# Attention projections of a two-layer kernel: eight block products replaced by seven, with weight sums prepared ahead

## The chip, the cores and the metric

The kernel runs on one core of one Trainium2 chip. The metric is the device time of one execution in microseconds (us). A kernel is run several times and the median counts; one more execution is recorded by the hardware profiler, and all durations below come from that one. The engines are named as in the profile: PE multiplies matrices, PEld is its weight load, DVE does elementwise work, ACT does elementwise functions, POOL and SP issue DMAs here.

## What is computed

Two attention layers follow each other, on four images of 32 x 32 tokens with 768 channels and 12 heads of 64. Cut to what matters:

```
for layer in (0, 1):
    xn  = group_norm(x)                    # 32 groups of channels
    q, k, v = xn @ Wq + bq, xn @ Wk + bk, xn @ Wv + bv
    if layer == 1:                         # depthwise 3x3 convolution and layer norm of each
        q, k, v = [layer_norm(dwconv3x3(t)) for t in (q, k, v)]
    a   = softmax(q @ k.T / 8 + rel_h(q) + rel_w(q))     # per image and head, 1024 x 1024
    o   = a @ v        (+ q in layer 1)
    x   = x + o @ Wp + bp                  # the projection that this change touches
```

All arrays are fp32. The projection of one image and layer is a product of a 768 x 768 matrix with 768 x 1024 outputs of attention (channels by tokens).

## The kernel before

All work stands in one long function, `two_layers`. Channels lie on the 128 partitions, so 768 channels are six tiles (NC = 6) of 128, and the 1024 tokens of an image are two halves of 512. A *stage* is one image in one layer. The eight stages run in the order: images 0 and 1 in layer 0, images 0 and 1 in layer 1, then images 2 and 3 likewise. A stage has six *pairs*, each a pair of heads (128 channels); 48 pairs in all, numbered from 0.

**The order is written out by hand.** PE, DVE, ACT and POOL execute exactly what the Python program emits, in that order; only SP's DMAs are placed by the scheduler. `attend` (L663) is a generator for one pair. For each half of the queries it does two groups of four key tiles: scores (L724, L726), exponentials (L731), running sums of them on DVE (L738, L740), then the product with V (L746), called AV here. It yields twice after the four score tiles and twice after AV, so a pair has 16 *steps*: steps 0 and 1 of each four stand between scores and AV, steps 2 and 3 between AV and the next scores. The dictionary `events` says what else is emitted at which step, relative to the start of a stage: Q, K and V of the next pair, convolution taps (L506, L508), norms, loads, mixes, projections. The loop at the end of `two_layers` walks through steps and events.

**PSUM** has eight banks: scores use one fixed double bank and two places (`place_b`, `place_c`) of two banks each; between scores these places are handed out as single banks by `bank` (L119) in a rotating order, with one further small bank that also serves the sum over keys, `z` (L688).

**Seven products for Q, K and V.** In layer 0, from the third pair on, `sevens` (L355) already computes two 128-channel blocks at once by seven products of quarters (Strassen's scheme): the contraction of six tiles is cut into two times three, the tokens into two halves. It needs five sums of token quarters (`mix_tokens`, L272) and five sums of weight quarters for each of nine pairs of blocks. `mix_weights` (L256) makes the latter once, in stage 0: it loads two weight tiles, writes each of five sums (L268) into a tile `x` of which there are two, and stores it to DRAM (`mixed`, L269). Loading and summing are emitted in the same step. The steps are listed near the end of `two_layers` (steps 2, 4, 18, 34, 36, 50, 56, 60, 66).

**The projection** `project` (L758) of stage k is emitted in stage k+1, in steps 7 to 14. For each of six output tiles m it loads the weights (L764), and for each half of the tokens it loads the residual x (L776), makes one product over six tiles of attention outputs (L131, called from L779, out tile `proj`), adds bias and residual on DVE (L780) and stores (L781). A product is six calls of `halves` (L128), each of which issues two matmuls of 128 x 64 weights with 512 columns; the profile lists each of these as two instructions. In layer 1 of image 0 a bias is first computed on PE from the weights (`pbias`, L770). The last stage's projection has no stage after it and is emitted after the last pair, with a check of all softmax sums (L838 to L844) in between; this stretch is called the tail below.

Of the kernel before, what the change touches and what calls it, by code (L numbers as in the profile page):

```python
# [9 lines left out]
F32 = mybir.dt.float32  # L10
# [3 lines left out]
ALU = mybir.AluOpType  # L14
# [3 lines left out]
P = 128  # L18
B = 4
S = 32  # L20
T = S * S
C = 768
NC = C // P
D = 64
HALF = T // 2
# [6 lines left out]
BIAS = (0, 24)  # L32
TAPS = 48
LN = 75
# [11 lines left out]
def two_layers(ctx: ExitStack, tc: tile.TileContext, keep, x_in, wqkv, wproj, rels, windows, vrow, small, const, onehot, picks, out):  # L46
# [19 lines left out]
    nc = tc.nc  # L66
    pool = lambda name, bufs, **kw: ctx.enter_context(tc.tile_pool(name=name, bufs=bufs, **kw))
    fixed = pool("fixed", 1)
    dram = pool("dram", 1, space=bass.MemoryType.DRAM)
    xnp = pool("xnp", 2)  # L70
    wp = pool("wp", 2)
    work = pool("work", 2)
    one = pool("one", 1)
# [45 lines left out]
    def bank(name):  # L119

        place = turn.pop(0)
        turn.append(place)
        return place.single(name) if place else small_bank(name)

    def small_bank(name):
        return ps_small.tile([P, 512], F32, tag="small", name=name)

    def halves(ps, a, b, start=True, stop=True, **kw):  # L128

        for lo in (0, D):  # L130
            nc.tensor.matmul(ps[lo : lo + D], a[:, lo : lo + D], b, start=start, stop=stop, **kw)  # L131
# [15 lines left out]
    def col(c, lo=0, hi=P):  # L147
        return sm[lo:hi, c : c + 1]
# [15 lines left out]
    stages = [(b0 + k, layer) for b0 in range(0, B, 2) for layer in range(2) for k in range(2)]  # L164
# [8 lines left out]
    weights = {}  # L173

    N_SUMS = 5
    mixed = [dram.tile([P, N_SUMS, NC // 2, P], F32, tag=f"mixed{u}", name=f"mixed{u}") for u in range(NC + NC // 2)]
    mixed_there = set()


# [3 lines left out]
    def part(at, n):  # L183
        return shared[:, at : at + n]
# [24 lines left out]
    for i, (_, layer, hp) in enumerate(items):  # L209
        first = (i - 1) * 16 + shift(i)  # L210
# [7 lines left out]

    def load_xn(stage):
        b, layer = stage  # L220
        xn = xnp.tile([P, NC, T], F32, tag="xn", name="xn")
        src = rows(mid[b] if layer else x_in[b])
        for n in range(NC):
            nc.sync.dma_start(xn[:, n, :], src[:, n, :])
        xns[stage] = xn

    def two(i, s):

        hp = items[i][2]
        return ((hp, 0), (hp, 1)) if s == 0 else ((hp, 2), (hp + 1, 2))  # L230

    def load_weights(n):

        if n >= len(uses):
            return
        i, s, *some = uses[n]
        _, layer, hp = items[i]
        w = wp.tile([P, NC, P], F32, tag="wqkv", name="wqkv_t")
        weights[uses[n]] = w
        if not some:  # L240
            nc.sync.dma_start(w, wqkv[layer, hp, :, s])
        elif some[0] == 0:
            (pa, sa), (pb, sb) = two(i, s)
            nc.sync.dma_start(w[:, :3, :], wqkv[0, pb, :, sb, 3:])
            nc.sync.dma_start(w[:, 3:, :], wqkv[0, pa, :, sa, :3])
        else:
            u = hp if s == 0 else NC + hp // 2
            assert u in mixed_there
            sums = slice(2 * some[0] - 2, min(2 * some[0], N_SUMS))
            n_sums = sums.stop - sums.start  # L250
            nc.sync.dma_start(w[:, : 3 * n_sums, :].rearrange("p (a n) c -> p a n c", n=3), mixed[u][:, sums])

    def used(use):
        load_weights(uses.index(use) + 2)

    def mix_weights(u):  # L256

        (pa, sa), (pb, sb) = two(u, 0) if u < NC else two(2 * (u - NC), 2)
        a = wp.tile([P, NC, P], F32, tag="wproj", name="mix_a")
        nc.sync.dma_start(a, wqkv[0, pa, :, sa])  # L260
        b = wp.tile([P, NC, P], F32, tag="wproj", name="mix_b")
        nc.sync.dma_start(b, wqkv[0, pb, :, sb])
        a1, a2, b1, b2 = a[:, :3, :], a[:, 3:, :], b[:, :3, :], b[:, 3:, :]
        sums = (b1, b2, ALU.add), (a1, a2, ALU.add), (a1, b2, ALU.add), (a2, b2, ALU.subtract), (b1, a1, ALU.subtract)
        for n, (x, y, op) in enumerate(sums):
            to = wp.tile([P, HALF], F32, tag="x", name="mix")
            to = to[:, : 3 * P].rearrange("p (n c) -> p n c", c=P)
            nc.vector.tensor_tensor(to, x, y, op)  # L268
            nc.sync.dma_start(mixed[u][:, n], to)  # L269
        mixed_there.add(u)  # L270

    def mix_tokens(stage):  # L272

# [53 lines left out]
    pbias = fixed.tile([P, NC], F32, tag="pbias", name="pbias")  # L327
# [333 lines left out]
    rest, found = [], ()  # L661
# [95 lines left out]

    def project(stage, os):  # L758

        b, layer = stage  # L760
        src, dst = rows(mid[b] if layer else x_in[b]), rows(out[b] if layer else mid[b])
        for m in range(NC):
            w = wp.tile([P, NC, P], F32, tag="wproj", name="wproj_t")
            nc.sync.dma_start(w, wproj[layer, :, :, m, :].rearrange("h p q -> p h q"))  # L764
            bias = col(BIAS[layer] + 18 + m)
            if layer:
                if b == 0:
                    ps = small_bank("pbias")
                    for n in range(NC):
                        nc.tensor.matmul(ps[:, 0:1], w[:, n, :], col(LN + 5), start=(n == 0), stop=(n == NC - 1))  # L770
                    nc.vector.tensor_tensor(pbias[:, m : m + 1], ps[:, 0:1], bias, ALU.add)
                bias = pbias[:, m : m + 1]
            for h in range(2):
                cols = slice(h * HALF, (h + 1) * HALF)
                x = wp.tile([P, HALF], F32, tag="x", name="x")
                nc.sync.dma_start(x, src[:, m, cols])  # L776
                ps = bank("proj")
                for n in range(NC):
                    halves(ps, w[:, n, :], os[n][:, cols], n == 0, n == NC - 1)  # L779
                nc.vector.scalar_tensor_tensor(x, ps, bias, x, ALU.add, ALU.add)  # L780
                nc.sync.dma_start(dst[:, m, cols], x)  # L781
                yield


    events = {}

    def at(step, piece):
        events.setdefault(step, []).append(piece)

    n_steps = NKT * (T // QC)  # L790
    oss = [[] for _ in stages]
    for k in range(1, len(stages)):
        first = (k - 1) * NC * n_steps
        at(first + n_steps, lambda k=k: load_xn(stages[k]))
        norm = group_norm(stages[k])
        for r in range(12):
            at(first + 2 * n_steps + 2 + 3 * r, lambda norm=norm: next(norm, None))
        if stages[k][1] == 0:
            mix = mix_tokens(stages[k])
            for r in range(5):  # L800
                step = 5 * n_steps + r // 3 if stages[k - 1][1] else 4 * n_steps + 4 + r // 2
                at(first + step, lambda mix=mix: next(mix, None))
        elif stages[k - 1][1] == 0:
            at(first + 4 * n_steps + 6, lambda: [nc.gpsimd.memset(pad, 0.0) for pad in pads])
    mix = mix_tokens(stages[0])
    for r in range(5):
        at(12 + r // 2, lambda mix=mix: next(mix, None))

    for u, step in ((2, 2), (7, 4), (3, 18), (4, 34), (8, 36), (5, 50), (0, 56), (6, 60), (1, 66)):
        at(step, lambda u=u: mix_weights(u))  # L810
    pairs = [Pair(i) for i in range(len(items))]
    for i, pair in enumerate(pairs):
        for r, piece in pair.plan():
# [1 line left out]
    for n in range(2):  # L815
        load_weights(n)
    for k, stage in enumerate(stages):
        steps = project(stage, oss[k])
        first = (k + 1) * NC * n_steps
        for r in range(2 * NC):  # L820
            at(first + 7 + 2 * r // 3, lambda steps=steps: next(steps, None))
    for _ in group_norm(stages[0]):
        pass
    for step in sorted(e for e in events if e < 0):
# [2 lines left out]
    step = 0  # L827
    for i, pair in enumerate(pairs):
        for _ in attend(pair, oss[i // NC]):
            for piece in events.pop(step, ()):  # L830
                piece()
            step += 1
    for part in rest:
        found = part(*found)
    def check():

        total = stat.tile([P, 1], F32, tag="total", name="total")
        nc.vector.tensor_reduce(total, seen, AX.X, ALU.add)  # L838
        good = stat.tile([P, 1], F32, tag="good", name="good")
        nc.vector.tensor_scalar(good, total, LIMIT, None, ALU.is_lt)  # L840
        ps = small_bank("good")
        nc.tensor.matmul(ps[:1, :1], cst[:, ONES : ONES + 1], good, start=True, stop=True)
        bad = keep.tile([1, 1], mybir.dt.int32, tag="bad", name="bad")
        nc.vector.tensor_scalar(bad, ps[:1, :1], -1.0, 1.0 * P, ALU.mult, ALU.add)  # L844
        return bad

    last = [piece for step in sorted(events) for piece in events.pop(step)]
    for piece in last[:2]:
        piece()
    bad = check()  # L850
    for piece in last[2:]:
        piece()
    for place in (place_b, place_c):
        place.close()
    return bad
# [288 lines left out]
```

## Time and profile before

| what | value |
|---|---|
| median of three runs | 3959.64 us (3958.61 to 3959.95) |
| the profiled execution's own time | 3959.69 us |
| its span | 3957.8 us |
| granted PE clock, mean | 0.997 |
| matmuls of the projection, `proj` | 2304 instructions |
| matmuls of Q, K and V by six tiles, `qkv` | 3648 instructions, 815.6 us busy |
| DVE: running sums of exponentials (L740) | 576, 705.6 us busy |
| DVE: convolution taps (L508) | 576, 758.4 us busy |
| DVE: bias and residual (L780) | 96, 72.1 us busy |
| load of projection weights | 48 of 384 KB, 3.7 us to landing |
| load of x from `mid`, store to `out` | 48 each of 256 KB, 2.7 and 3.2 us to landing |
| store of x to `mid` | 48 of 256 KB, 3.7 us to landing |
| load of weight sums | 66 of 384 KB, 3.1 us, and 33 of 192 KB, 2.3 us |

A line of groups in the profile reads: line of the kernel, engine, operation, output tile <- input tiles, shape, count | busy us, mean ns of one | idle time of the engine just before, and what ended it. Matmuls overlap each other, so the mean of one (593 ns) is longer than the distance from one to the next. A line of windows has the length of the window, then for PE, PEld, DVE, ACT and POOL the busy us with the number of instructions, then granted clock, share of the DMA engines and GB/s. A line of the timeline has the start, the duration, the instructions, and in brackets how long the engine had been idle and who ended that.

### The profile page before, as it was taken

How to read it: one execution, taken by the hardware profiler on the slowest of the kernel's cores; microseconds unless marked ns; L12 is line 12 of the kernel's file. 1: busy time of each engine (PE TensorE's matmuls, PEld its weight loads, DVE VectorE, ACT ScalarE, POOL GpSimd, SP SyncE). 2: the span in 40 equal slices, each digit the busy share in tenths (PEclk: the TensorE clock that was granted, in tenths of full speed). 3: DMA queues.
4: the chain of work that ended last, by engine and by line, in shares of the span. 5: the costliest groups of instructions: out<-in, count | busy, mean ns of one | idle time of the engine just before them, and what ended most of it. 6: DMA issues, size and time to landing. Idle time of an engine off the chain costs nothing.

```text
span 3957.8 us, 79930 instructions
## 1 busy us (share of the span) xinstructions
PE 3884.8 (98%) x35026; PEld 1743.2 (44%) x35026; DVE 2492.4 (63%) x2794; ACT 1835.7 (46%) x2717; POOL 411.4 (10%) x776
## 2 busy tenths in 40 slices
PE   7999999999999999999899999999999999999999
PEld 3535534534344444444445355355443444434443
DVE  2456424558489984799633554245675998848883
ACT  2454424555255552455423554254542555525551
POOL 0111100110000100000011110001100011000010
PEclk9999999999999999999999999999999999999999
DMA  5333242221411312212133222423124112131122
GB/s 161 85 115 113 77 135 75 65 55 50 130 46 35 87 43 84 62 44 70 43 104 90 59 72 64 147 59 76 44 59 124 38 46 52 44 103 44 38 48 76
DMA packets 179044, 293.33 MB, mean 74 GB/s; under 512 B 22528, under 2 KB 77952, under 8 KB 178688
## 3 DMA queue, kind: packets, MB, share of 16 engines
q1 hardware_dynamic: 117248, 187.41, 15.1%
q0 software_dynamic: 61440, 100.71, 11.1%
q8 instruction: 279, 4.57, 0.5%
q14 instruction: 77, 0.63, 0.1%
HBM read 153.36 MB, written 34.01 MB: 47 GB/s over the span
## 4 chain that ended last, share of the span: by engine, by line
PE 88%; DVE 9%; DMA 1%; issue 1%; ACT 0%; POOL 0%; DVEq 0%; SPq 0%; ACTq 0%
PE qkv L131 18%; PE s L724 16%; PE av L746 15%; PE proj L131 13%; PE m3m L131 4%; PE s L726 4%; PE m1m L131 4%; PE m4m L131 4%; DVE shared L508 3%; PE rel L566 3%; PE ln_c L131 3%; PE z L688 2%; DVE acc L740 2%; PE m L131 2%; PE ln_t L544 1%
## 5 line engine op out<-in xcount | busy, mean ns | idle before, releaser
L731 ACT ACTIVATE e<-s 128x1024 f32<-128x1024 f32 x768 | 776.1, 1024 | 447.5 <-PE s L726 414.0
L131 PE MATMUL qkv<-xn,wqkv_t 128*64 128x512 f32 x3648 | 815.6, 597 | 7.2 <-DVE gmean L300 4.1
L740 DVE TENSOR_TENSOR acc<-acc,e 128x1024 f32<-128x1024 f32 x576 | 705.6, 1225 | 183.7 <-ACT e L731 132.7
L724 PE MATMUL s<-q,k 64*128 64x512 f32 x3072 | 810.8, 604 | 4.3 <-ACT e L731 3.5
L508 DVE SCALAR_TENSOR_TENSOR shared<-shared,sm 128x1056 f32<-128x1056 f32 x576 | 758.4, 1317 | 14.9
L726 PE MATMUL s<-bias,ones 64*128 64x512 f32 x1536 | 612.8, 790 | 10.0 <-DMA bias<-high 7.1
L746 PE MATMUL av<-e,vt 128*64 128x512 f32 x2624 | 594.2, 595 | 0.0
L593 POOL DMA_DIRECT2D bias<-high x384 | 204.2, 552 | 3271.6 <-ACT high L582 3023.5
L131 PE MATMUL proj<-q,wproj_t 128*64 128x512 f32 x2304 | 504.2, 593 | 0.2 <-DVE bad L844 0.2
L131 PEld LDWEIGHTS qkv<-xn,wqkv_t 128*64 128x64 f32 x3648 | 253.9, 137 | 491.8 <-issue 481.4
L491 ACT ACTIVATE shared<-qkv,sm 128x512 f32<-128x512 f32 (+1 forms) x288 | 129.1, 502 | 595.8 <-PE qkv L131 595.8
L724 PEld LDWEIGHTS s<-q,k 64*128 64x128 f32 x3072 | 281.9, 187 | 257.8 <-issue 217.0
L746 PEld LDWEIGHTS av<-e,vt 128*64 128x64 f32 x2624 | 185.0, 137 | 346.9 <-issue 320.1
L131 PEld LDWEIGHTS proj<-q,wproj_t 128*64 128x64 f32 x2304 | 163.3, 137 | 316.6 <-issue 315.8
L738 DVE TENSOR_TENSOR acc<-e 128x1024 f32<-128x1024 f32 x96 | 117.5, 1224 | 293.7 <-ACT e L731 282.4
L726 PEld LDWEIGHTS s<-bias,ones 64*128 64x128 f32 x1536 | 150.2, 188 | 195.2 <-issue 183.6
L593 POOL DMA_DIRECT2D bias<-whole x384 | 206.4, 567 | 125.4 <-DVE whole L583 115.8
L681 ACT COPY weighed<-av 128x512 f32<-128x512 f32 x96 | 56.3, 586 | 301.9 <-PE av L746 301.9
L780 DVE SCALAR_TENSOR_TENSOR x<-proj,sm,x 128x512 f32<-128x512 f32 x48 | 36.1, 751 | 217.0 <-PE proj L131 217.0
L780 DVE SCALAR_TENSOR_TENSOR x<-proj,pbias,x 128x512 f32<-128x512 f32 x48 | 36.0, 751 | 215.8 <-PE proj L131 215.8
L131 PEld LDWEIGHTS ln_c<-cst,shared 128*64 128x64 f32 x2304 | 133.3, 139 | 50.2 <-issue 42.3
L131 PE MATMUL ln_c<-cst,shared 128*64 128x128 f32 x2304 | 141.4, 277 | 8.2 <-DVE shared L508 7.5
(121 smaller groups left out, 3744.0 us busy)
## 6 DMA issues: line engine op xcount, KB each, us to landing
bias<-high POOLq DMA_DIRECT2D x384, 128.0 KB, 2.8
bias<-whole POOLq DMA_DIRECT2D x384, 128.0 KB, 3.0
wqkv_t<-in_wqkv SPq DMA_DIRECT2D x78, 384.0 KB, 3.1
wqkv_t<-mixed SPq DMA_DIRECT2D x66, 384.0 KB, 3.1
wproj_t<-in_wproj SPq DMA_DIRECT2D x48, 384.0 KB, 3.7
wqkv_t<-in_wqkv SPq DMA_DIRECT2D x66, 192.0 KB, 2.5
xn<-in_x SPq DMA_DIRECT2D x24, 512.0 KB, 7.7
x<-in_x SPq DMA_DIRECT2D x48, 256.0 KB, 2.8
```

Source lines behind the costliest of these rows:

```text
L131: nc.tensor.matmul(ps[lo : lo + D], a[:, lo : lo + D], b, start=start, stop=stop, **kw)
L491: nc.scalar.activation(self.pad[s][:, rows, there : there + src.shape[2]], src, AF.Identity, bias=col(self.column(s)))
L508: nc.vector.scalar_tensor_tensor(y, window, tap, y, ALU.mult, ALU.add)
L566: nc.tensor.matmul(ps[lo : lo + S, k * S : (k + 1) * S].rearrange("p (b c) -> p b c", b=2), rel[rows, 2 * self.layer + i, first : first + ...
L593: nc.gpsimd.dma_start(sets, some.unsqueeze(1).to_broadcast([D // 2, 2, QC]))
L688: nc.tensor.matmul(z[j * D : (j + 1) * D, :], cst[:, ONES : ONES + D], acc[:, j, :], start=True, stop=True,)
L724: nc.tensor.matmul(ps[:, j, :], k[rows, keys], q[rows, cols], start=True, stop=False)
L726: nc.tensor.matmul(ps[:, j, :], ones[rows, keys], bias[c][rows, kt // 2, :], start=False, stop=True,)
L731: nc.scalar.activation(e, ps, AF.Exp)
L738: nc.vector.tensor_tensor(acc, es[0], es[1], ALU.add)
L740: nc.vector.tensor_tensor(acc, acc, e, ALU.add)
L746: nc.tensor.matmul(av[j * D : (j + 1) * D, :], pair.vt[:, kt, j * D : (j + 1) * D], e[:, j, :], start=(kt == 0), stop=(kt == NKT - 1),)
```

## The change

The projection takes the form that `sevens` has, for two output tiles at once (`four` and `three` are its first four and last three products), and the sums of weights are made differently.

- `project` now returns three things: a call that loads the first weights, `sums`, which forms 15 sums of 128 x 512 attention outputs on DVE (nine into new space, six in place), and `products`, a generator that emits `four` and `three` for three pairs of output tiles.
- Each product is three calls of `halves`. `four` accumulates products 1 and 3 in one bank and 2 and 4 in another; ACT copies the bank after product 1, DVE adds it after product 2. `three` accumulates products 5 and 7 in one bank, DVE adding it in between, and 6 in another. A pair of output tiles has four DVE adds for the shared terms and two more in the final additions.
- The steps: in stages followed by layer 0, sums at steps 4 to 6 and products at 7, 9, 11, 13, 14, 15; in those followed by layer 1, sums at 1, 6, 8, 9, 10 and products at 9, 11, 13, 15, 17, 19. In the last stage the sums of two of three heads are put at steps 4 and 6 of the last pair, one more at step 10, and the rest after it.
- The new space is the input buffer of the same stage, which is free by then: `xnp` has two tags of one buffer in place of one tag of two. The load of the next input goes from step 16 to step 20 of a stage.
- `mix_weights` handles six more pairs of weight blocks, those of the projection (9 to 11 for layer 0, 12 to 14 for layer 1). The load is emitted some five steps ahead of the sums. Three of the five sums are written in place over their operands and stored from there. The bias `pbias` is computed there, in stage 1.

```
-    for u, step in ((2, 2), (7, 4), (3, 18), (4, 34), (8, 36), (5, 50), (0, 56), (6, 60), (1, 66)):
-        at(step, lambda u=u: mix_weights(u))
+    for u, call, step in (
+        (2, 0, 5), (7, 6, 11), (3, 13, 18), (4, 22, 29), (8, 31, 38), (5, 40, 47), (0, 49, 55), (6, 57, 63), (1, 65, 71),
+        (9, 72, 77), (10, 78, 83), (11, 84, 89), (12, 138, 143), (13, 145, 150), (14, 152, 157),
+    ):
+        mix = mix_weights(u)
+        for at_step in (call, step):
+            at(at_step, lambda mix=mix: next(mix))
...
-        sums = (b1, b2, ALU.add), (a1, a2, ALU.add), (a1, b2, ALU.add), (a2, b2, ALU.subtract), (b1, a1, ALU.subtract)
-        for n, (x, y, op) in enumerate(sums):
-            to = wp.tile([P, HALF], F32, tag="x", name="mix")
-            to = to[:, : 3 * P].rearrange("p (n c) -> p n c", c=P)
+        for n, to, x, y, op in (
+            (2, None, a1, b2, ALU.add), (4, None, b1, a1, ALU.subtract), (0, b1, b1, b2, ALU.add),
+            (1, a1, a1, a2, ALU.add), (3, a2, a2, b2, ALU.subtract),
+        ):
+            if to is None:
+                to = wp.tile([P, HALF], F32, tag="x", name="mix")
+                to = to[:, : 3 * P].rearrange("p (n c) -> p n c", c=P)
             nc.vector.tensor_tensor(to, x, y, op)
             nc.sync.dma_start(mixed[u][:, n], to)
...
-            for h in range(2):
-                cols = slice(h * HALF, (h + 1) * HALF)
-                x = wp.tile([P, HALF], F32, tag="x", name="x")
-                nc.sync.dma_start(x, src[:, m, cols])
-                ps = bank("proj")
-                for n in range(NC):
-                    halves(ps, w[:, n, :], os[n][:, cols], n == 0, n == NC - 1)
-                nc.vector.scalar_tensor_tensor(x, ps, bias, x, ALU.add, ALU.add)
-                nc.sync.dma_start(dst[:, m, cols], x)
+        def m(ps, pair, at, x, some=range(3), more=False):
+            w = weights[4 * pair + at // 2][:, 3 * (at % 2) : 3 * (at % 2) + 3, :]
+            for n in some:
+                halves(ps, w[:, n, :], x(n), start=not (n or more), stop=n == 2, skip_group_check=True)
...
+        def put(which, cols, x, ps, term=None):
+            bias = pbias[:, which : which + 1] if layer else col(BIAS[0] + 18 + which)
+            nc.vector.scalar_tensor_tensor(x, ps, bias, x, ALU.add, ALU.add)
+            if term is not None:
+                nc.vector.tensor_tensor(x, x, term, ALU.add)
+            nc.sync.dma_start(dst[:, which, cols], x)
...
+        def four(pair, n_first=3):
+
+            u, w = extra(9), extra(10)
+            b1, b2 = bank("p4p2"), bank("p3p5")
+            x21, x12 = get(2 * pair + 1, first), get(2 * pair, second)
+            m(b1, pair, 0, extra)
+            nc.scalar.copy(u, b1)
+            yield
+            m(b2, pair, 1, lambda n: extra(n + 3), range(n_first))
+            if n_first == 3:
+                add(u, u, b2)
+            m(b1, pair, 2, x11, more=True)
+            m(b2, pair, 1, lambda n: extra(n + 3), range(n_first, 3))
+            load(4 * pair + 2)
+            if n_first < 3:
+                add(u, u, b2)
+            add(w, u, b1, ALU.subtract)
+            put(2 * pair + 1, first, x21, b1)
+            m(b2, pair, 3, x22, more=True)
+            load(4 * pair + 3)
+            add(u, u, b2, ALU.subtract)
+            put(2 * pair, second, x12, b2)
+            yield
+
+        def three(pair):
+            u, w = extra(9), extra(10)
+            b3, b4 = bank("p1p6"), bank("p7")
+            x11, x22 = get(2 * pair, first), get(2 * pair + 1, second)
+            m(b3, pair, 4, lambda n: extra(n + 6))
+            add(u, u, b3)
+            m(b4, pair, 5, lambda n: os[n + 3][:, first])
+            load(4 * pair + 4)
+            put(2 * pair, first, x11, b4, u)
+            m(b3, pair, 6, lambda n: os[n][:, second], more=True)
+            load(4 * pair + 5)
+            put(2 * pair + 1, second, x22, b3, w)
...
+        if k + 1 == len(stages):
+            at(first - 12, call)
+            for r, *what in ((-12, range(5), (0,)), (-10, range(5), (1,)), (-6, (0,), (2,))):
+                at(first + r, lambda sums=sums, what=what: sums(*what))
+            continue
+        at(first + 2, call)
+        late = stages[k + 1][1]
+        for r, what in ((1, (0,)), (6, (1,)), (8, (2,)), (9, (3,)), (10, (4,))) if late else ((4, (0, 1)), (5, (2,)), (6, (3, 4))):
+            at(first + r, lambda sums=sums, what=what: sums(what))
+
+        for r, n in zip((9, 11, 13, 15, 17, 19) if late else (7, 9, 11, 13, 14, 15), (2, 1) * 3):
+            for _ in range(n):
+                at(first + r, lambda products=products: next(products))
...
+    found = rest.pop(0)(*found)
+    next(products)
     for part in rest:
         found = part(*found)
+    sums(range(1, 5), (2,))
```

`get` loads a residual tile, `load` the next weights into one of two buffers, `extra(i)` is the i-th 128 x 512 part of the new space, and `add` is a DVE addition.

## The prediction on record

> **What bounds the kernel.** I read the page's busy shares first, then the granted clock, then TensorE (PE) cut by head pair, then PE's waits. A "pair" is one of the 48 rounds of attention over two heads; its start is its first exponential, and the windows below are such rounds.
>
> ```profile
> PE 3884.8 (98%) x35026; PEld 1743.2 (44%) x35026; DVE 2492.4 (63%) x2794; ACT 1835.7 (46%) x2717; POOL 411.4 (10%) x776
> L131 PE MATMUL proj<-q,wproj_t 128*64 128x512 f32 x2304 | 504.2, 593 | 0.2 <-DVE bad L844 0.2
> ```
>
> PE is idle 73 us of 3957.8. "Busy" may hide slack, so I look at pairs with and without projection (columns: window, length, then busy of PE, weight load, DVE, ACT, POOL):
>
> ```profile
> 476.90:593.70 116.80, 116.80 (x798) 42.57 (x796) 35.40 (x39) 32.64 (x42) 8.31 (x16) 1.00 0.41 122
> 666.90:722.20 55.30, 55.30 (x513) 22.34 (x512) 33.38 (x40) 32.42 (x42) 6.41 (x13) 1.00 0.20 54
> 947.90:1085.20 137.30, 137.30 (x970) 53.83 (x968) 74.68 (x86) 44.02 (x71) 8.30 (x16) 1.00 0.34 103
> 1085.20:1160.50 75.30, 75.30 (x682) 33.21 (x680) 65.77 (x69) 42.98 (x69) 8.31 (x16) 1.00 0.22 59
> ```
>
> A layer-0 pair that carries a projection is 61.5 us longer than one that does not; in layer 1 it is 62.0. DVE has 62.6 us idle in the third window. So PE work in a projection is time, one for one. Its price is in the tail, where nothing else runs (chain of what ended last):
>
> ```profile
> 3900.56 51.74 PE proj L131 x240
> ```
>
> 51.74/240 = 0.2156 us an instruction. A stage's projection has 12 products x 6 heads x 2 halves x 2 instructions = 288, so 62.1 us, agreeing with the windows.
>
> **Part 1: seven products for eight.** Per stage: 3 pairs of output blocks x 7 products x 3 heads x 2 halves x 2 = 252 instructions, 36 fewer: 36 x 0.2156 = **7.76 us**. For the seven stages that run beside attention this is 54.3 us, if PE doesn't wait. Whether it waits is the question, since the new form lets ACT or DVE read a PSUM bank in the middle of its accumulation. The kernel already does this for Q and K (PE, a pair of stage 1; 12 instructions a product):
>
> ```profile
> 671.01 2.75 PE L131 MATMUL m4m<-xn,wqkv_t 128*64 128x512 f32 x12
> 673.58 2.75 PE L131 MATMUL m3m<-xn,wqkv_t 128*64 128x512 f32 x12
> 676.16 2.74 PE L131 MATMUL m4m<-xn,wqkv_t 128*64 128x512 f32 x12
> 678.73 2.74 PE L131 MATMUL m3m<-xn,wqkv_t 128*64 128x512 f32 x12
> ...
> 684.74 2.75 PE L131 MATMUL m1m<-shared,wqkv_t 128*64 128x512 f32 x12
> 687.32 2.75 PE L131 MATMUL m<-shared,wqkv_t 128*64 128x512 f32 x12
> 689.89 2.75 PE L131 MATMUL m1m<-shared,wqkv_t 128*64 128x512 f32 x12
> 692.57 1.13 PE L724 MATMUL s<-q,k 64*128 64x512 f32 x4
> ```
>
> Starts are 2.58 us apart: no gap at either reuse of a bank. [...]
>
> The sequence gives each reader one product's time: product 3 into bank 1 needs only ACT's copy, which has product 2 as cover; product 4 into bank 2 needs one DVE add (0.69), covered by product 3, so DVE may be 2.58 - 0.69 = 1.9 us behind; the last product likewise.
>
> *DVE's own load.* Added per stage: 15 sums of outputs and 3 x 6 adds = 33 of about 0.69 (row L707, 0.692), 22.8 us. The 12 final adds stay. In layer 0: 35 + 23 of 109 us. In layer 1: 75 + 23 of 129 us. The tightest place is the first product group of a layer-1 pair (event step 9). By my addition of rows from the pair's start, DVE ends its norm 5.8 us after PE starts the scores, then owes three acc adds (3.8), four tap steps (4.7) and six sums (4.2): it is free 18.5 us after those scores started. PE meanwhile has scores 4.4, z 1.0, centring 1.8, one padded product 5.2, transposes 2.2 and two short products 5.2, 19.8. The add is due a product later: about 3 us in hand. Later groups have more. ACT gains three copies of 0.59 a stage.
>
> *What it does cost in waits.* PE's waits at such products, from 480 to 3890 us:
>
> ```profile
> PE m4m L131 <- issue: 4.5, 3, 3.0
> PE m3m L131 <- DVE shared L376: 0.5, 1, 0.5
> ```
>
> 5.0 us over 25 groups of seven, 0.2 each, most of it in one group at the DVE-bound end of a layer-1 stage. I take 21 groups x 0.2 = **4 us** loss. Bounds: 0, and 12 layer-1 groups at that worst group's 3.6 us, 43 us.
>
> *SP's queue.* Per pair of blocks it issues five weight loads, four x loads and four stores in order, and x loads wait for a store to land (3.2 to 3.7 us), with weight loads behind them. The tightest weight load is freed after product 2 and needed after product 4: 5.2 us for a landing of 3.1. Beside attention, AV (3.4) or scores (4.4) add slack. I charge nothing; if the cover went, about 0.5 us a load.
>
> *Moves.* The next input load goes from step 16 to 20 of a stage, 14 steps (some 65 us) ahead of its first reader; its landing is 4.2 to 7.7, and on SP it stands behind the projection's last stores, which it needs in any case. POOL's queue gets nothing. One buffer for each parity now holds the sums; its last reader is step 19. The 9.0 us of bias matmuls (72 x 0.25, window 1465.8 to 1612.4 is that much longer) only move to stage 1. Nothing.
>
> **Part 2: sums of weights.** Today each of nine mixes writes five tiles through two buffers:
>
> ```profile
> DVE mix L268 <- DMA mixed<-mix: 31.6, 18, 3.9
> ```
>
> That is DVE's waits; then PE's timeline at the first long stall, and the window around it, whose last three columns are granted clock, DMA share and GB/s:
>
> ```profile
> 232.81 4.49 PE L131 MATMUL m1m<-shared,wqkv_t 128*64 128x512 f32 x12 [2.77 <-DVE shared L376]
> ```
>
> ```profile
> 231.00:239.00 8.00, 6.19 (x24) 2.08 (x24) 2.53 (x4) 2.71 (x4) 0.00 (x0) 0.79 0.72 213
> ```
>
> DVE stands for 31.6 us; where Q's adds are queued behind, PE stands too: 2.77 at 232.8, 2.98 at 321.2, 0.42 at 290.9 and 371.6, and 1.43 at 359.8, half of which I put down to it. And the two long ones are followed by a lower clock: 0.79 over 8 us is 1.7 us lost, and the 12 matmuls took 4.49, not 2.75, so 1.74 each. With three sums in place only two tiles need a buffer, both free long before. 2.77 + 2.98 + 0.84 + 0.7 + 2 x 1.74 = 10.8; I take **10.5 us**. Bounds: 5 (the new steps meet other adds) and 13 (all stalls there go). Six more mixes add 30 x 0.56 on DVE where it is under half busy.
>
> **Part 3: the tail.** 7.76 us goes there too, but comes back, because nothing covers DVE.
>
> ```profile
> 3882.10 5.20 DVE L740 TENSOR_TENSOR acc<-acc,e 128x1024 f32<-128x1024 f32 x4
> 3887.36 1.08 PE L688 MATMUL z<-acc,cst 128*64 128x512 f32 x4 [0.44 <-DVE acc L740]
> ```
>
> In the last pair DVE would end ten sums (7.2) at 3877.4 where its acc began at 3875.46; with one more sum the acc ends 2.75 later and z waits about 3.2. A 2.77 wait halved the clock and 2.41 (at 3853, clock 1.00) did not, so I count a dip, net 1.2 after later waits absorb some. Product 4 waits for four sums and an add: 1.3. The check's matmul waits 0.7 longer. Two first weight loads of a group, freed one product ahead, come some 0.4 late each. The last output takes one add more, 0.7. 7.76 - 2.75 - 1.2 - 1.3 - 0.7 - 0.8 - 0.7 = 0.3; I take **0.5** (from -3 to +4). [...]
>
> **Sum.** 54.3 - 4 + 10.5 + 0.5 = 61.3. The profiled execution took 3959.69, 1.89 over its span, and stands beside the median 3959.64. 3959.69 - 61.3 = **3898**.
>
> **Rivals.**
> *A. DVE falls behind in layer 1.* In layer-1 pairs without projection it is busy 65.8 of 75.3, and two groups now run up to step 19, in the second pair. If each of 12 groups there loses 1 to 2.6 us (the last: the whole gain): 12 to 31 us, less the 4 charged: 3906 to 3925. For: 87% busy. Against: after each product group DVE waits for PE anyway (4.4 us before each output add today).
> *B. Stage 0 keeps its stalls.* The mixes still stand in DVE's queue, now fifteen: 10.5 falls to 0 to 5: 3904 to 3909. Against: the waits named are all for stores that aren't needed any more.
> *C. Slower.* DVE stands between products everywhere: 21 groups with three places each (product 4, last product, next scores that reuse the bank), 63 in all. The gain is gone once each costs 65/63 = 1.0 us, that is, once DVE is 1.9 + 1.0 = 2.9 us behind at every one. At 1.5 us: 3959.7 - 65 + 95 = 3989. Against: 25 groups at 0.2.
> *D. Better.* No flow stalls, 13 in stage 0, 4 in the tail: 3888.
>
> **Chances.** Forecast with D 0.74 (own range 3886 to 3905), A 0.15, B 0.07, C 0.04. The range 3885 to 3921 takes in D, B and most of A. About 0.2% (8 us) is what a measurement can tell from no change: faster 0.95, same 0.01, slower 0.04.
>
> **What would show it.** Pair 6 near 109 us for 116.8; pairs 12 and 13 together near 205 for 212.6; 2016 projection instructions for 2304; no wait of DVE's mix for stores, and PE's stalls between 130 and 380 us nearly gone; a wait of about 3 us at the last z, with a stretch of lower clock behind it. I am wrong if PE waits for DVE at the products of stages 2, 3, 6 and 7 for more than a microsecond a group, or for weights after SP's x loads.

## The result, and the profile after

The changed kernel takes 3921.53 us (median of 4 runs, 3918.14 to 3922.39) against 3959.77 for the kernel before beside it: a ratio of 0.9902, 95% interval 0.9885 to 0.9920, so 38 us faster. 61 us were forecast: the time lies outside the forecast's own range (3886 to 3905) and at the very end of the range that takes in the rivals (3885 to 3921). The profiled execution took 3920.75, its span is 3918.9, that is 38.9 less than before.

The page's busy shares of the changed kernel:

```profile
PE 3835.0 (98%) x34738; PEld 1726.2 (44%) x34738; DVE 2673.5 (68%) x3088; ACT 1850.3 (47%) x2741; POOL 411.7 (11%) x776
```

PE has the 288 instructions less that were announced (8 stages x 36) but sheds only 49.8 us of busy time, where 288 x 0.2156 would be 62.1. So some other PE work became slower. Cut by head pairs (window, length, then busy of PE, weight load, DVE, ACT and POOL; the last three columns are granted clock, DMA share and GB/s):

```profile
464.00:573.50 109.50, 109.40 (x762) 39.92 (x760) 55.99 (x72) 34.51 (x46) 8.30 (x16) 1.00 0.41 120
...
647.60:711.40 63.80, 61.54 (x536) 27.94 (x534) 36.84 (x50) 32.39 (x43) 8.28 (x16) 0.94 0.25 66
711.40:802.10 90.70, 85.95 (x896) 49.09 (x896) 40.08 (x57) 34.74 (x48) 9.67 (x16) 0.93 0.38 108
952.90:1066.10 113.20, 111.76 (x850) 45.08 (x848) 92.08 (x112) 44.90 (x72) 8.31 (x16) 1.00 0.30 84
1066.10:1159.50 93.40, 93.40 (x766) 39.05 (x764) 69.12 (x76) 43.65 (x71) 8.27 (x16) 1.00 0.38 116
3811.30:3918.90 107.60, 93.60 (x421) 32.62 (x418) 55.82 (x74) 25.73 (x36) 1.70 (x4) 0.94 0.30 94
```

The rows are pairs 6, 8, 9, 12, 13 and 47. Pairs 9 and 47 before, which the prediction does not show:

```profile
722.20:797.00 74.80, 73.75 (x848) 40.76 (x847) 35.07 (x46) 34.29 (x47) 11.33 (x20) 1.00 0.28 74
3854.00:3957.80 103.80, 96.21 (x456) 33.94 (x452) 34.76 (x41) 23.93 (x33) 1.92 (x4) 1.00 0.26 81
```

Pairs 6, 12 and 13 are nearly as forecast (109.5 for 116.8, with 109 forecast; 206.6 together for 212.6, with 205 forecast). Pairs 8 and 9, which carry no projection, are longer than before: 63.8 for 55.3 and 90.7 for 74.8, with a granted clock of 0.94 and 0.93. The last pair with the tail is longer too, 107.6 for 103.9, also at 0.94.

The whole difference, by starts of pairs (us, after less before):

| part | before | after | difference | forecast |
|---|---|---|---|---|
| to pair 6 (start and stage 0) | 476.9 | 464.0 | -12.9 | -10.5 |
| stage 1, pairs 6 to 11 | 471.0 | 488.9 | +17.9 | +1.2 (7.8 off, 9.0 moved in) |
| stage 3, pairs 18 to 23 | 523.6 | 508.8 | -14.8 | -16.8 (9.0 moved out) |
| stages 2, 4, 5, 6 and 7 to pair 47 | | | -32.9 | -34.8 (five times 7.8 off, and all of the 4 us of waits put here) |
| pair 47 and tail | 103.9 | 107.6 | +3.7 | -0.5 |

PE's waits in the changed kernel (total, times, longest), the rows that are new:

```profile
PE p1p L131 <- DVE os_sums L845: 5.8, 4, 1.5
PE pbias L281 <- DVE pbias L282: 3.7, 3, 3.2
PE pbias L281 <- DVE gmean L324: 2.0, 1, 2.0
PE good L972 <- DVE good L970: 2.0, 1, 2.0
PE z L712 <- DVE acc L764: 1.8, 1, 1.8
PE p3p L131 <- DVE os_sums L845: 0.9, 1, 0.9
```

Six microseconds of waits at the bias matmuls do not make 17. The rest is seen in PE's timeline of pairs 8 and 9:

```profile
703.44 2.51 PE L281 MATMUL pbias<-sm,mix_a 128*128 128x1 f32 x12 [2.00 <-DVE gmean L324]
706.20 2.72 PE L281 MATMUL pbias<-sm,mix_b 128*128 128x1 f32 x12 [0.25 <-DVE pbias L282]
...
787.69 1.50 PE L281 MATMUL pbias<-sm,mix_a 128*128 128x1 f32 x12
792.37 2.68 PE L281 MATMUL pbias<-sm,mix_b 128*128 128x1 f32 x12 [3.19 <-DVE pbias L282]
794.98 5.76 PE L770 MATMUL av<-e,shared 128*64 128x512 f32 x16
```

A group of 12 takes 1.50 at one place and 2.5 to 2.7 at others, and the AV product behind the last one 5.76 where it takes 3.65 elsewhere. In the rows of the granted clock it is 0.5 for 10.24 us from 703.7, for 3.41 from 751.5 and for 6.83 from 792.4: 20.5 us at half rate, about 10.2 us of work lost. Such a stretch at half clock is called a dip below. Before, the same groups stood directly in front of two products, and the granted clock was 1.00 from 1489 to 1504:

```profile
1493.55 1.50 PE L770 MATMUL pbias<-sm,wproj_t 128*128 128x1 f32 x12
1494.97 5.37 PE L131 MATMUL proj<-q,wproj_t 128*64 128x512 f32 x24
```

So 17.9 = -7.3 (projection) + 9.0 (the matmuls at their old speed) + 16.2, and of the 16.2 the half clock makes 10.2 and the waits (2.00, 0.25, 0.25, 3.19) 5.7. That is my theory, still read from one trace. The rival: the three mixes that moved here (loads, DVE sums, stores) cost it themselves, and the clock only follows.

### The profile page after: what moved, and what is told of

Its sections match the earlier page's. It is cut to its first block, busy times and chain, and to the rows that moved or that the text cites. A ratio compares the mean times of both kernels' runs of the same rounds, so it can differ in the third digit from the quotient of the medians.

```text
span 3918.9 us, 79880 instructions
## 1 busy us (share of the span) xinstructions
PE 3835.0 (98%) x34738; PEld 1726.2 (44%) x34738; DVE 2673.5 (68%) x3088; ACT 1850.3 (47%) x2741; POOL 411.7 (11%) x776
## 4 chain that ended last, share of the span: by engine, by line
PE 86%; DVE 11%; DMA 1%; issue 1%; ACT 1%; POOL 0%; DVEq 0%; SPq 0%; ACTq 0%
PE qkv L131 18%; PE s L748 15%; PE av L770 15%; PE m4m L131 4%; PE m3m L131 4%; PE m1m L131 4%; PE s L750 4%; DVE shared L532 3%; PE p3p L131 3%; DVE acc L764 3%; PE p1p L131 3%; PE p4p L131 3%; PE ln_c L131 3%; PE rel L590 3%; PE z L712 2%; PE m L131 2%
## 5 line engine op out<-in xcount | busy, mean ns | idle before, releaser
L748 PE MATMUL s<-q,k 64*128 64x512 f32 x3072 | 817.1, 609 | 4.3 <-ACT e L755 3.5
L750 PE MATMUL s<-bias,ones 64*128 64x512 f32 x1536 | 617.0, 796 | 10.9 <-DMA bias<-high 7.5
L748 PEld LDWEIGHTS s<-q,k 64*128 64x128 f32 x3072 | 283.2, 188 | 263.2 <-issue 216.8
L750 PEld LDWEIGHTS s<-bias,ones 64*128 64x128 f32 x1536 | 150.8, 189 | 199.2 <-issue 191.6
L590 PEld LDWEIGHTS rel<-q,rel 64*32 64x32 f32 x6144 | 111.7, 105 | 78.0 <-issue 58.7
L131 PE MATMUL m4m<-xn,wqkv_t 128*64 128x512 f32 x528 | 122.4, 599 | 4.0 <-issue 3.0
L400 DVE TENSOR_TENSOR shared<-shared,m3m 128x512 f32<-128x512 f32 x66 | 45.4, 687 | 118.3 <-PE m3m L131 118.2
L590 PE MATMUL rel<-q_t,rel 64*32 64x32 f32 x6144 | 123.3, 195 | 2.3 <-issue 2.3
```

The costliest lines, as they stand in the source:

```text
L590: nc.tensor.matmul(ps[lo : lo + S, k * S : (k + 1) * S].rearrange("p (b c) -> p b c", b=2), rel[rows, 2 * self.layer + i, first : first + ...
L748: nc.tensor.matmul(ps[:, j, :], k[rows, keys], q[rows, cols], start=True, stop=False)
L750: nc.tensor.matmul(ps[:, j, :], ones[rows, keys], bias[c][rows, kt // 2, :], start=False, stop=True,)
```

## The experiments

Times are medians beside the kernel before of the same chip (3959.1 to 3959.9). Runs of one changed kernel spread over 1 to 5 us, so a difference of 1 or 2 us between two of them says nothing.

### Without the bias matmuls

```
-                ps = small_bank("pbias")
...
-                nc.vector.tensor_tensor(pbias[:, m + i : m + i + 1], ps[:, 0:1], col(BIAS[1] + 18 + m + i), ALU.add)
+                nc.vector.tensor_copy(pbias[:, m + i : m + i + 1], col(BIAS[1] + 18 + m + i))
```

> The changed kernel without the 72 bias matmuls of mixes 12 to 14: pbias is copied from the bias column, so the term that those matmuls add is left out. Theory (the bias groups, moved away from the projection's products, cost PE waits and half clock around them): their own 9.0 us and the 16.2 us that stage 1 lost beyond them go, 3921.5 - 25 = about 3896; stage 1 (pairs 6 to 11) takes 464 us for 489, and no granted clock under 1.0 stands between 600 and 900 us. Rival (the 16.2 us come from the mixes themselves: their loads, their DVE adds, their stores): only the 9.0 us go, 3912, stage 1 takes 480, and pairs 8 and 9 stay longer than in the kernel before.

Measured: 3893.78, ratio 0.9832 (0.9816 to 0.9849), 27.8 below the changed kernel. Stage 1 takes 464.3. Pairs 8 and 9, with all three mixes still in them:

```profile
649.20:704.40 55.20, 55.20 (x512) 22.30 (x510) 33.36 (x40) 32.39 (x43) 6.39 (x13) 1.00 0.21 53
704.40:778.40 74.00, 73.84 (x848) 41.67 (x846) 40.75 (x63) 34.25 (x47) 11.40 (x20) 1.00 0.44 123
```

55.2 and 74.0, the lengths of before, at clock 1.00. The loads, sums and stores of the mixes are all still there. The rival falls: the mixes are free, the bias matmuls are not.

### Both groups in one bank

```
-                ps = small_bank("pbias")
+            ps = small_bank("pbias")
...
+                    nc.tensor.matmul(ps[:, i : i + 1], w[:, n, :], col(LN + 5), start=(n == 0), stop=(n == NC - 1))
+            for i in range(2):
+                nc.vector.tensor_tensor(pbias[:, m + i : m + i + 1], ps[:, i : i + 1], col(BIAS[1] + 18 + m + i), ALU.add)
```

> The changed kernel with the two bias groups of a mix in two columns of one PSUM bank, back to back, and DVE's two adds behind both; steps unchanged. The waits between the groups go (0.25 + 0.25 + 3.19 = 3.7 us); the wait of 2.0 for the group norm's mean stays. Theory, in two forms that part here: if only idle time of PE halves the clock, the second and third mix (3.0 us of one-column matmuls without a wait) show full clock, and the time is about 3912; if one-column matmuls count for the clock like idle time, both still show a dip of 3.4 us, and the time is about 3915. Rival (the clock dips have nothing to do with these groups): 3918, with the dips where they were and as long.

Measured: 3911.66, ratio 0.9883 (0.9866 to 0.9899). By the time alone the form "idle time only" would be right; by the clock's rows neither is. Dips stand at 709.4 and 750.4, 3.41 us each; the third mix has none. The dip at 750.4 follows 2.9 us of one-column matmuls in which PE never waits:

```profile
746.57 1.50 PE L281 MATMUL pbias<-sm,mix_a 128*128 128x1 f32 x12
747.93 1.48 PE L281 MATMUL pbias<-sm,mix_b 128*128 128x1 f32 x12
750.67 2.08 PE L749 MATMUL s<-q,k 64*128 64x512 f32 x4
```

The scores behind it start at half rate (2.08 for 1.13). So half clock came here without a wait; and the same 2.9 us at 786.6 cost nothing, the AV product behind them took its 3.65. What decides between the two is not shown: behind the first stand 1.3 us of position matmuls of 32 columns, behind the second that product.

### The groups at two steps

```
                 nc.vector.tensor_tensor(pbias[:, m + i : m + i + 1], ps[:, 0:1], col(BIAS[1] + 18 + m + i), ALU.add)
+                if i == 0:
+                    yield
...
-        (9, 72, 77), (10, 78, 83), (11, 84, 89), (12, 138, 143), (13, 145, 150), (14, 152, 157),
+        (9, 72, 77), (10, 78, 83), (11, 84, 89), (12, 117, 124, 126), (13, 130, 139, 141), (14, 146, 156, 158),
```

> The changed kernel with each mix of 12 to 14 in three steps: a call, the first bias group, and the second with the sums; the two groups have an attention product of 3.6 us or more between them, and none stands behind the group norm's mean or in front of the small position matmuls. Theory: no wait at a bias group over 0.5 us, no half clock between 600 and 900 us, 3921.5 - 16 = about 3905, stage 1 about 473. Rival (the mixes themselves): within 3 us of the changed kernel, since they are all still there.

Measured: 3904.99, ratio 0.9866 (0.9849 to 0.9882), 16.5 below the changed kernel with the same work done. Stage 1 takes 472.9, which is 471.0 - 7.3 + 9.0 = 472.7 within 0.2. Pairs 8 and 9 stand at full clock, without a wait at a bias group:

```profile
651.20:709.30 58.10, 58.10 (x538) 25.18 (x536) 37.61 (x50) 32.41 (x42) 8.30 (x16) 1.00 0.32 88
709.30:786.40 77.10, 76.66 (x872) 43.45 (x870) 36.43 (x51) 34.29 (x48) 9.33 (x16) 1.00 0.33 90
```

The loads and sums of the mixes moved to other steps too, but without the bias matmuls they had cost nothing at the old ones. So the whole 16.2 was a matter of where the groups stood.

### Wide bias matmuls at the old places

```
-                    nc.tensor.matmul(ps[:, 0:1], w[:, n, :], col(LN + 5), start=(n == 0), stop=(n == NC - 1))
+                    nc.tensor.matmul(ps, w[:, n, :], col(LN + 5).to_broadcast([P, 512]), start=(n == 0), stop=(n == NC - 1))
```

> The changed kernel with its bias groups at their places and behind their waits, but each matmul 512 columns wide (the same column read 512 times by a broadcast), so that 12 instructions take 12 x 0.2156 = 2.6 us for 1.5. [...]

Measured, in two runs only: 3932.45, ratio 0.9931 (0.9911 to 0.9951). The size put in for a wide instruction was wrong: with its 128 x 128 weight tile it takes 0.45 here (5.44/12), not 0.2156, so a group takes 5.44 and six groups add 6 x (5.44 - 1.50) = 23.6 us, not the 6.5 of 2.6 a group. Stage 1 is only 11.0 longer than in the changed kernel (499.9 for 488.9), so 12.6 came back, about the 10.2 of half clock and the 3.19 that the longer groups now cover. The clock's rows show from where: no half rate at all between 600 and 900 us, although the wait of 2.0 is still there:

```profile
702.92 5.44 PE L281 MATMUL pbias<-sm,mix_a 128*128 128x512 f32 x12 [2.01 <-DVE gmean L324]
708.61 5.44 PE L281 MATMUL pbias<-sm,mix_b 128*128 128x512 f32 x12 [0.25 <-DVE pbias L282]
```

From 700.3 to 710.5 PE is busy for 7.94 us in both kernels, and the granted clock is 0.67 in the changed one and 1.00 in this one. At the second mix the waits are alike too. A stretch of 3.41 us that holds the wait of 0.25 between its groups, and the 3.42 us behind it, first in the changed kernel and then in this one (granted clock third from the end):

```profile
748.07:751.48 3.41, 3.16 (x145) 3.02 (x146) 1.52 (x5) 0.17 (x1) 0.00 (x0) 1.00 0.02 5
751.48:754.90 3.42, 3.42 (x12) 1.39 (x10) 2.00 (x7) 2.89 (x5) 0.00 (x0) 0.50 0.67 238
```

```profile
753.75:757.16 3.41, 3.16 (x8) 1.25 (x7) 0.16 (x1) 0.00 (x0) 0.00 (x0) 1.00 0.00 0
757.16:760.58 3.42, 3.42 (x16) 1.22 (x18) 0.00 (x0) 0.00 (x0) 0.00 (x0) 1.00 0.00 0
```

PE counts as busy for 3.16 us in both. In the changed kernel 1.7 us of that are one-column matmuls, most of the rest position matmuls of 32 columns, and half clock follows; here all of it is 512 columns wide, and none follows. So at this place the half clock went with the narrow matmuls and not with the wait between the groups.

### Part 2 alone

```
-    for u, step in ((2, 2), (7, 4), (3, 18), (4, 34), (8, 36), (5, 50), (0, 56), (6, 60), (1, 66)):
-        at(step, lambda u=u: mix_weights(u))
+        (2, 0, 5), (7, 6, 11), (3, 13, 18), (4, 22, 29), (8, 31, 38), (5, 40, 47), (0, 49, 55), (6, 57, 63), (1, 65, 71),
...
+        (2, None, a1, b2, ALU.add), (4, None, b1, a1, ALU.subtract), (0, b1, b1, b2, ALU.add),
```

> The kernel before with part 2 alone: its nine mixes called ahead, with three sums in place and two through buffers, at the steps of the changed kernel; projection, input loads and bias matmuls as before. Theory (stage 0's stalls were DVE waiting for stores): what the changed kernel shows up to pair 6, 12.9 us, is all of it: 3959.7 - 13 = about 3947, no PE stall over 0.5 us between 220 and 380 us. Rival (part of that gain came with the other edits, as the later input load or the buffers): my 10.5 or less, down to 3955.

Measured: 3949.41, ratio 0.9976 (0.9967 to 0.9986): 10.4 us, with an interval from 5.5 to 13. By the time that is the rival's figure, but the profile gives the theory's: from its first pair to pair 6 stage 0 takes 401.6 for 414.1, that is 12.5 less (11.9 less in the changed kernel), and PE's waits for DVE between 220 and 380 us are gone. So the gain of part 2 stands by itself. Which of its three edits makes it, the sums in place, the earlier loads or the new steps, this run does not show.

### The second group of seven in layer 1

The four waits of 1.44 at the seventh product come from DVE's queue. DVE around the first (its idle time in brackets), and PE's product:

```profile
1056.69 0.17 DVE L157 TENSOR_TENSOR t_ln<-r_ln 128x16 f32<-128x16 f32 x1 [5.75 <-ACT r_ln L155]
...
1061.25 0.68 DVE L845 TENSOR_TENSOR os_sums<-os_sums,p1p 128x512 f32<-128x512 f32 x1
```

```profile
1061.98 2.79 PE L131 MATMUL p1p<-q,wproj_t 128*64 128x512 f32 x12 [1.44 <-DVE os_sums L845]
```

The add that frees the bank stands behind V's norm, which waits 5.75 for ACT. It is an idle DVE that comes late. The edit, on the kernel of split groups:

```
-        for r, n in zip((9, 11, 13, 15, 17, 19) if late else (7, 9, 11, 13, 14, 15), (2, 1) * 3):
+        for r, n in zip((9, 11, 13, 14, 17, 19) if late else (7, 9, 11, 13, 14, 15), (2, 1) * 3):
```

> The kernel of split bias groups with one number more: in layer-1 stages the last three products of the second group of seven are issued at step 14 for 15, so ahead of V's norm. Theory (PE's 1.44 at the seventh product, once in each of four stages, is DVE's add standing behind that norm, which waits for ACT): the four waits go, 3905.0 - 5.8 = about 3899. Rival (DVE is simply full there): the wait only moves, to V's transposes or to the next scores, and the time is 3903 or more; worse than 3907 if the norm now comes late for AV.

Measured: 3896.69, ratio 0.9841 (0.9825 to 0.9857), 8.3 below the kernel of split groups. Pair 12:

```profile
936.90:1048.40 111.50, 111.50 (x850) 45.18 (x848) 87.76 (x105) 44.84 (x72) 8.30 (x16) 1.00 0.30 86
```

111.5 for 113.2, PE never idle; four such pairs make 6.7, so the theory holds. In the profiled execution the last pair is shorter too (103.3 for 107.8), since there is no half clock at its start or behind the check; that part is not the edit's.

### DVE's order in the tail

```
-            for r, *what in ((-12, range(5), (0,)), (-10, range(5), (1,)), (-6, (0,), (2,))):
+            for r, *what in ((-17, range(5), (0,)), (-10, range(5), (1,)), (-6, (0,), (2,))):
...
-    sums(range(1, 5), (2,))
+    sums((1,), (2,))
```

> The kernel of split bias groups with DVE's order changed in the last stage alone: the five sums of head 0 are issued before the last pair (DVE is idle there for 8 us), and of the last head's sums three are issued behind the product that needs none of them. Theory (the tail lost its gain to DVE's order): z's wait falls from 1.8 to 0.4 and the wait at the fourth product from 1.1 to under 0.4: 3905.0 - 2.2 = about 3903. Rival (ACT's chain from the sums of z to its inverse sets the end in any case): PE's waits only move behind z, no gain over 0.5 us.

Measured: 3906.07, ratio 0.9864 (0.9847 to 0.9880): no gain. z waits 1.2 for 1.8, the fourth product 0.86 for 1.1, and then:

```profile
3848.83 0.19 PE L976 MATMUL good<-good,cst 128*1 128x1 f32 x2 [3.19 <-DVE good L974]
3849.26 5.39 PE L131 MATMUL p1p<-os_sums,wproj_t 128*64 128x512 f32 x12 [0.24 <-DVE bad L978]
```

The check's wait grows from 2.0 to 3.2, since two sums now stand ahead of it, and the product behind runs at half rate. My theory of the tail fell. The rival's time held, but not its reason: the wait that grew is for DVE's sums, and that ACT's chain sets the end is not shown.

### The check of the tail in two parts

```
         nc.vector.tensor_scalar(good, total, LIMIT, None, ALU.is_lt)
+        yield
         ps = small_bank("good")
...
+            x = wp.tile([P, NC, P], F32, tag="wqkv", name="x") if last else wp.tile([P, HALF], F32, tag="x", name="x")
```

> The kernel of split bias groups with the check of the tail in two parts (DVE's sum where it was, PE's one-column matmul four products later) and two buffers of another kind for the last two x tiles. Theory (the tail's loss is the check's wait, the half clock behind it, and the last x load that waits for a store): the waits of 2.0 and 0.24 and the dip of 1.7 go, the end comes 1.2 earlier: 3905.0 - 5 = about 3900. Rival (the time goes into the next wait, for weights, or the dip comes anyway, from the waits at z and at the fourth product): gain under 2.

Measured: 3899.34, ratio 0.9851 (0.9834 to 0.9867), 5.7 below the kernel of split groups. The last pair takes 101.4 for 107.8, of which 1.5 is not the edit's: half clock covers 2.4 us of its start for 5.4, ahead of what the edit changes; the profile of the kernel with step 14 for 15 has none there. PE at the check in the kernel of split groups, and then the same products now:

```profile
3846.12 0.19 PE L974 MATMUL good<-good,cst 128*1 128x1 f32 x2 [1.99 <-DVE good L972]
3846.55 4.49 PE L131 MATMUL p1p<-os_sums,wproj_t 128*64 128x512 f32 x12 [0.24 <-DVE bad L976]
```

```profile
3841.57 2.80 PE L131 MATMUL p3p<-q,wproj_t 128*64 128x512 f32 x12 [1.11 <-DVE os_sums L848]
3844.20 2.75 PE L131 MATMUL p1p<-os_sums,wproj_t 128*64 128x512 f32 x12
...
3855.07 0.19 PE L977 MATMUL good<-good,cst 128*1 128x1 f32 x2
```

No wait, and 2.75 for the 4.49 that also the changed kernel shows behind its check: 2.0 + 0.24 + 1.7 = 3.9. At the end DVE waited 2.27 for the last x in the changed kernel (1.91 in the kernel of split groups); now it waits 1.10, for PE, so the earlier x load is worth 1.2 (0.8). The two lines, of the changed kernel and of this one:

```profile
3911.67 0.75 DVE L840 SCALAR_TENSOR_TENSOR x<-p1p,pbias,x 128x512 f32<-128x512 f32 x1 [2.27 <-DMA x<-mid]
```

```profile
3889.77 0.75 DVE L843 SCALAR_TENSOR_TENSOR x<-p1p,pbias,x 128x512 f32<-128x512 f32 x1 [1.10 <-PE p1p L131]
```

The runs of the two kernels do not overlap, but nearly touch (3898.8 to 3903.4 and 3903.5 to 3906.5). That the half clock is gone may not be the edit's alone, as the kernel with step 14 for 15 lacks it in its profile without this edit; that the wait of 2.0 is gone is the edit's.

### Together

> Split bias groups, the layer-1 order of step 14, the tail's check in two parts with two more x tiles, and the tail's sums in the new order, together. If the gains stand beside each other: 3905.0 - 6.6 (layer-1 order, 4 x 1.65 in the pairs) - 6.4 (check and x, by the last pair's length) = 3892, and the sums' order, alone worth nothing since the check's wait took it, now gives 1 more: 3891. If the sums' order only moves waits also here: 3892 or a little above.

> The same without the new order of the tail's sums: 3905.0 - 6.6 - 6.4 = 3892 by the sum of the parts. If parts overlap (the same window of the clock saved twice): up to 3895. Against the kernel with all of it, this tells whether the order of the sums is worth the 1 us of z's shorter wait.

Measured: 3891.69 (ratio 0.9829, 0.9816 to 0.9843) with all four edits, 3893.13 (0.9831, 0.9818 to 0.9845) without the order of the sums. Within the spread of the runs the parts add up, although the 6.4 put in for the tail held 1.5 that is not the edit's. The order of the sums cannot be told from nothing. 3891.7 is 29.8 below the changed kernel.

## Why the prediction was off in size

The direction and the main terms held; the gain was 38.9 of the span where 61.3 was forecast. By my steps:

- **"The 9.0 us of bias matmuls ... only move to stage 1. Nothing."** This is the step that failed: they cost 16.2 us more there. The 9.0 itself is right as six groups of 1.50; the "72 x 0.25" beside it is not, since the 0.25 of one instruction overlaps the next, and it would make 18. I had priced 72 instructions by their row and not looked at what stood on either side. Three things were in reach. Their bank is also the group norm's, so a DVE copy stands between (2.0). The second group waits for DVE's add of the first, and DVE had a running sum of exponentials (5.2) and a norm (1.5) ahead of it, so PE waited 3.19. And in front of a product they left the clock at 1.00; among waits it was 0.5 for 20.5 us.
- **Part 1, flow: 54.3 - 4.** Measured 46.0. Where layer 0 follows, the reuse of banks costs next to nothing, as the row of Q and K said (stages 4 and 5 gain 7.3 and 7.7 of 7.76); rival A was right in kind (DVE late in layer 1) and wrong in place: not the full DVE of the last group but the order at step 15 of the second, 5.8 us by the waits, 6.7 by the pairs of the experiment. My "later groups have more" in hand was worked out by DVE's load; what counted was an instruction ahead that waits for ACT.
- **Part 2: 10.5.** A little low: stage 0 is 11.9 shorter in the changed kernel and 12.5 with part 2 alone. That the medians with part 2 alone give 10.4 is chance, within their interval. The 12.9 to pair 6 hold 1.0 of an earlier first pair.
- **Part 3: 0.5.** Measured -3.7. z's wait was put too high: 1.8, so 1.4 more than before, and no dip behind it (2.75 more and 1.2 for the dip were forecast). Fourth product (0.9 for 1.3), the check's wait (0.6 longer for 0.7) and weights (0.55 for 0.8) were about right. Not seen: the half clock behind the check (4.49 - 2.75 = 1.7); and the end, where PE's last product ends 8.5 before the span's end for 5.6 before, 2.9 for the 0.7 that I gave to one more add. Of these, 1.2 is the last x load, which waits for a store; about 1.0 behind the last add I can't place. Half clock at the pair's start (to 3816.65, so 5.3 us, 2.7 lost) was in no term. With 1.4 for z, these make 10.8, less 7.76: 3.0 of the 3.7. In the profile of the kernel with step 14 for 15, which has the same tail and neither stretch of half clock, the last pair takes 103.3 for 103.9 before. So the loss in the tail differs by over 4 us between executions, and that 0.6 comes near the forecast 0.5 is chance, as the terms were others.

Against the 61.3, the terms that came out otherwise are -4.3 (flow), +2.4 (stage 0), -16.2 (bias) and -4.2 (tail), which gives 39.0. That the time came out at the end of the range on record is luck: its upper part stood for rival A, which cost 6.7 and not 12 to 31, and the 16.2 stood in no term.

## What to carry to other kernels

A group of narrow matmuls has no price of its own: here it was 1.5 us in front of a wide product and 4.2 on average among waits ((9.0 + 16.2) / 6), so when one is moved, look at what PE does just ahead of it and just behind it, and at who else uses its bank. An engine's load alone did not say here whether it would be late; look for the one instruction ahead in its queue that waits for a third engine. When a wait is taken out of a chain, look for the next instruction there that waits for the same engine: in the tail the check took all that z gave back.

## What the runs showed of the hardware

The length of a wait did not tell by itself whether half clock came with it. Before, PE waited 0.43 and then 2.41, up to 3853.45, in front of scores (L724, L726), and the granted clock was 1.00 from 3850 to 3856. In the changed kernel it waited 0.43 and then 2.40, up to 3810.51, in front of the same matmuls (L748, L750), and the clock was 0.5 from 3809.8 to 3816.65. What parts the two is not shown, so a price for a wait of 2 to 3 us, as the 1.2 for a dip at z, was an estimate: behind z's wait of 1.8 there was none, and behind the check's 1.99 the next product took 4.49 for 2.75.

Nor did the busy time of PE tell it. With its waits of 2.0 and 0.25 the first mix had PE busy for 7.94 of 10.2 us in one-column and in broadcast form, at a clock of 0.67 and of 1.00; the second, with a wait of 0.25, for 3.16 of 3.41 us in both, and 3.41 us at half clock came behind the narrow form alone. With both groups in one bank, 2.9 us of one-column matmuls without a wait were followed by half clock at 750.4, and the same at 786.6 were not. In these kernels the half clock at the mixes went away with wide groups and with groups placed apart (1.00 in pairs 8 and 9 of both); what in the narrow ones brought it, the runs do not part further. The page of the changed kernel says 98% busy, and pair 9 in it has PE busy for 85.95 of 90.70 us at a clock of 0.93.
